# Two reorderings in a two-layer graph attention kernel: two reductions ahead of a waiting step on VectorE, and four coarse gathers ahead of two fine ones on GpSimd

## The chip, the cores and the metric

The kernel runs on one core of a Trainium2 chip. The metric is the device time of one execution in microseconds (us), as the median of several runs. A profiled execution gives, besides, the time of every instruction. Five engines work side by side, each through its own instructions in order: PE (matmul), DVE (vector), ACT (activation), POOL (GpSimd) and SP, which here only issues DMAs. They meet at semaphores. POOL issues the indirect DMAs.

## The reference, cut to what matters

There are 16 graphs ("batches") of 1024 nodes with 256 features, and one adjacency matrix for all. Layer 0 is a small network with two attentions, layer 1 one more attention, each with a layer norm in front and a residual:

```python
out = relu(h @ mlp1_w + mlp1_b)          # 1024 x 512
out = elu(gat(out, None, W_fc, a_fc)) + out       # dense: every node sees every node
out = relu(out @ mlp2_w + mlp2_b)        # 1024 x 256
x = x + relu(elu(gat(out, adj, W_hand, a_hand)) + out)
x = x + relu(gat1(relu(layernorm(x)), adj, W, a))
# gat: e = leaky_relu(f1[i] + f2[j]); softmax over j (of the neighbours); att @ h; elu
```

The change concerns how the dense attention gets its result, and when layer 1 computes two extremes.

## The kernel before, in words

**Dense attention without a 1024 x 1024 product.** The exponential of a leaky ReLU of f1[i] + f2[j] is one of two products of a function of i and a function of j, depending on whether f2[j] lies over -f1[i]. So the kernel sorts the nodes by f2 (it counts ranks and scatters the rows of `h_nat` to DRAM, `sorted`), makes running sums of the sorted rows from both ends, and reads for every node i the two sums at its place. The sums are held in two tables in DRAM: a fine one (`fine`, sums within groups of eight rows) and a coarse one (`coarse`, sums over whole groups, made by two triangular products `carry` on PE). A node's sum is its fine row plus its coarse row. `gather` (L627 on) fetches them: for a half h of the nodes (512, four tiles of 128) and a tile u, a fine gather writes 128 rows of 1026 floats into `got`, and a coarse gather adds 128 rows to the same place in flight:

```python
nc.gpsimd.indirect_dma_start(
    out=got[u // n][:, u % n, :], out_offset=None,
    in_=(coarse_d if coarse else fine_d)[self.b % 2][:, :],
    in_offset=bass.IndirectOffsetOnAxis(ap=self.k[:, coarse, t:t + 1], axis=0),
    **({"compute_op": OP.add} if coarse else {}))
```

So a batch has sixteen gathers, eight per half, and a coarse one waits until the fine one of its tile has landed. `share` (L649 to L652, DVE) turns the four sums of a half into weights `den`, and so waits for the last coarse gather of its half. `mean` makes per tile `part` on ACT (L659) and `hp` on DVE (L661). `merge` (L708 on) turns the four `hp` of a half by PE transposes `hpT`, four times (c = 0 to 3), applies the elu (L710 on DVE, L711 and L712 on ACT, L718 on DVE), and POOL adds the result to `resT` (L719). Then comes the second product, `m` at L726. `hp` has four buffers, so both halves share them.

**Layer 1 and its extremes.** For each batch, `second_norm` turns the normalised rows (`nt`, L282), `project` makes `hmb` (PE products `pb` at L322, ACT copies at L324, a POOL memset of a column of ones at L318), and `extremes` (L329, L330) takes the largest and smallest of a column of eight numbers on each partition. `vectors` begins with a PE transpose `extpsb` (L238) that spreads the largest over the partitions. In steady batches the weighted product `ob` of layer 1 follows in the next batch's time.

**What sets the order.** Every step is entered in a table with a planned time, by `at(lo, hi, steps)`. The steps are sorted by that time, and the instructions of PE, DVE, ACT and SP are issued in just this order. POOL keeps the order of the table too, but for the scatters. The planned times are only places in a list; nothing waits for a clock. Batches overlap: the sums, gathers and merges of batch b + 1 run while batch b is in its masked attention and layer 1. A batch's place in the table is `base`, 142 planned us from the next. For batches from the second to the last, the fine gathers stand at `base + 44.5` and `base + 48`, the coarse ones at `base + 55` and `base + 62`; the shares at `base + 78` and `base + 91.4`; the reductions at `lo + 7.5` with `lo = base + 71`. Between the gathers POOL has other work: the two adds `posa` (L408) and `ea` (L409) of each tile of the masked attention of layer 0, whose result DVE adds to x (L413), and the inverse root of the next norm (`rstd`, L267 and L268), on which the centring `hn` (L272) waits.

On SP, the store of a finished half of the output (L429) and the load of a later x (L86) are issued in the time of the coarse gathers. They go through another DMA queue to the same sixteen DMA engines.

## Time and profile before

| | us |
|---|---|
| three runs: median (lowest to highest) | 2363.75 (2357.47 to 2365.26) |
| the profiled execution, its own time | 2357.62 |
| its span, from the first to the last instruction | 2355.9 |
| PE busy | 2264.0 |
| DVE busy | 1610.9 |
| ACT busy | 1243.7 |
| POOL busy | 954.7 |
| a fine gather on POOL, a coarse one (median) | 0.96, 1.55 |
| from a gather's issue to its landing (median) | 8.1 |
| one extreme, L329 or L330 (DVE) | 0.16 |

A line of the timeline reads: start in us from the span's start, duration in us, engine, line of the code, operation, result <- operands, their shapes, how many were merged into the line, and in brackets how long the engine stood idle before it and what ended that. A line of waits reads: who waited, for whom, us in total, times, longest. Busy time on PE is partly modelled. What POOL shows of a gather is its issue; the transfer goes on afterwards in the DMA engines. The mean granted clock of PE was 0.990.

### The profile page before, as it was taken

To read this page: it belongs to the slowest core of one execution; us is meant where nothing else is said; L and a number is where in the kernel's file an instruction comes from. 1 tells how busy PE (TensorE), PEld (TensorE's weight loads), DVE (VectorE), ACT (ScalarE), POOL (GpSimd) and SP (SyncE) were. 2 spreads that over 40 slices of the span, in tenths; PEclk is the share of its full clock that TensorE was granted. 3 is DMA by queue.
4 is the path that set the end of the run, shared out by engine and by line. 5 is a ranking of instruction groups with operands and counts; after the bars stand their busy time and mean duration, and the time that the engine had idled before them with its cause. 6 is when DMAs were issued, how large, how long until landed. Compare 5 with 4: busy or idle time off the path is not lost. (4 is left out here: it accounts for less than half of the span.)

```text
span 2355.9 us, 30815 instructions
## 1 busy us (share of the span) xinstructions
PE 2264.0 (96%) x9955; PEld 1750.0 (74%) x9955; DVE 1610.9 (68%) x4499; ACT 1243.7 (53%) x2740; POOL 954.7 (41%) x1216
## 2 busy tenths in 40 slices
PE   8989999999999999999999999999999999999897
PEld 6666777777868778787877868777786877778676
DVE  6666685766858577685866767586685857668554
ACT  5355645647365564745546374554736556473442
POOL 1153435264433536434263533535344352634320
PEclk9999999999999999999999999999999999999898
DMA  4558356572655746366573645657264564636500
GB/s 175 166 161 206 74 167 172 168 189 96 191 127 175 184 149 183 96 193 151 170 188 128 178 112 173 163 170 201 96 196 118 171 179 152 184 95 193 122 1 29
DMA packets 150762, 355.81 MB, mean 151 GB/s; under 512 B 11112, under 2 KB 62648, under 8 KB 146496
## 3 DMA queue, kind: packets, MB, share of 16 engines
q1 hardware_dynamic: 103968, 189.58, 26.4%
q0 software_dynamic: 45952, 163.99, 26.3%
q8 instruction: 82, 1.34, 0.2%
q14 instruction: 88, 0.72, 0.1%
q10 hardware_dynamic: 672, 0.17, 0.0%
HBM read 227.40 MB, written 126.30 MB: 150 GB/s over the span
## 5 line engine op out<-in xcount | busy, mean ns | idle before, releaser
L384 PE MATMUL ob<-hmb,attb 128*128 128x257 f32 x2048 | 466.7, 386 | 13.6 <-DVE attb L373 13.5
L465 PE MATMUL h<-wfc_sb,resT 128*128 128x257 f32 x2048 | 465.5, 380 | 0.0
L384 PE MATMUL oa<-hma,atta 128*128 128x258 f32 x2048 | 454.4, 382 | 3.1 <-DVE atta L373 2.9
L384 PEld LDWEIGHTS ob<-hmb,attb 128*128 128x128 f32 x2048 | 388.3, 192 | 79.1 <-ACT rb L422 12.5
L384 PEld LDWEIGHTS oa<-hma,atta 128*128 128x128 f32 x2048 | 387.1, 190 | 65.1 <-DVE atta L373 9.6
L465 PEld LDWEIGHTS h<-wfc_sb,resT 128*128 128x128 f32 x2048 | 379.4, 190 | 53.5 <-issue 0.7
L719 POOL TENSOR_TENSOR resT<-resT,e 128x512 f32<-128x512 f32 x128 | 163.3, 1276 | 386.9 <-DVE e L718 343.4
L408 POOL TENSOR_TENSOR posa<-posa,onat 128x256 f32<-128x256 f32 x120 | 100.8, 840 | 468.2 <-ACT posa L400 467.6
L373 DVE SCALAR_TENSOR_TENSOR atta<-rowsa,qwda,edge 128x256 f32<-128x256 f32 x512 | 268.2, 554 | 24.0 <-PE oa L384 12.6
L373 DVE SCALAR_TENSOR_TENSOR attb<-rowsb,qwdb,edge 128x256 f32<-128x256 f32 x512 | 237.2, 505 | 9.9 <-PE ob L384 7.4
L451 PE MATMUL m<-hT,w_sb 128*128 128x512 f32 x512 | 236.2, 599 | 0.5 <-ACT posa L400 0.5
L726 PE MATMUL m<-resT,w_sb 128*128 128x512 f32 x512 | 231.5, 599 | 4.4 <-POOL resT L719 4.4
L422 ACT ACTIVATE rb<-ob,recb 128x256 f32<-128x256 f32 x128 | 59.1, 475 | 332.1 <-DVE recb L420 320.4
L637 POOL DMA_INDIRECT got<-coarse,k x124 | 198.1, 1598 | 39.0 <-issue 35.4
L399 ACT ACTIVATE ea<-oa,reca 128x256 f32<-128x256 f32 x128 | 60.8, 475 | 267.6 <-DVE reca L396 267.6
L710 DVE TENSOR_SCALAR e<-hpT 128x512 f32<-128x512 f32 x128 | 88.4, 690 | 141.3 <-PE hpT L708 108.8
L726 PEld LDWEIGHTS m<-resT,w_sb 128*128 128x128 f32 x512 | 94.1, 192 | 107.2 <-issue 91.3
L451 PEld LDWEIGHTS m<-hT,w_sb 128*128 128x128 f32 x512 | 93.0, 194 | 92.1 <-issue 89.7
L637 POOL DMA_INDIRECT got<-fine,k x124 | 128.9, 1040 | 55.4 <-DMA fine<-xs 23.9
L525 POOL DMA_INDIRECT sorted<-hnat,place x128 | 131.4, 1026 | 39.5 <-issue 20.3
L548 ACT ACTIVATE junk<-r,fs 128x1024 int8<-128x1024 f32 x124 | 142.4, 1149 | 5.7 <-POOL fs L469 4.7
L711 ACT ACTIVATE e<-e 128x512 f32<-128x512 f32 x128 | 80.7, 631 | 88.0 <-DVE e L710 87.9
(186 smaller groups left out, 3442.4 us busy)
## 6 DMA issues: line engine op xcount, KB each, us to landing
xs<-sorted SPq DMA_DIRECT2D x32, 1028.0 KB
fine<-tt SPq DMA_DIRECT2D x32, 1026.0 KB
fine<-xs SPq DMA_DIRECT2D x32, 1026.0 KB
x<-in_x_dram SPq DMA_DIRECT2D x16, 1024.0 KB
out_dram<-x SPq DMA_DIRECT2D x32, 512.0 KB
xn<-in_x_dram SPq DMA_DIRECT2D x15, 1024.0 KB
coarse<-carry SPq DMA_DIRECT2D x32, 256.5 KB
r<-row_r SPq DMA_DIRECT2D x14, 512.0 KB
```

What stands on the lines that cost most here:

```text
L373: nc.vector.scalar_tensor_tensor(a_t, self.rows[:, q * PAIR:(q + 1) * PAIR], self.qwd[:, 1, j:j + 1], edge[:, j, q * PAIR:(q + 1) * PAIR], ...
L384: nc.tensor.matmul(self.out[t][:, :F + self.ONES], lhsT=self.att[q, j][:, (t % 2) * P:(t % 2 + 1) * P], rhs=self.hm[:, j, 2:2 + F + self.O ...
L408: adder.tensor_add(pos, pos, o_nat[:, t, :])
L451: nc.tensor.matmul(ps, lhsT=w1_sb[:, kc, c * P:(c + 1) * P], rhs=hT[:, kc, h * HALF:(h + 1) * HALF], start=(kc == 0), stop=(kc == FC - 1))
L465: nc.tensor.matmul(ps[:, :F + 1], lhsT=self.resT[:, kc, t * P:(t + 1) * P], rhs=wfc_sb[:, kc, g, :], start=(kc == 0), stop=(kc == HC - 1))
L525: made = nc.gpsimd.indirect_dma_start(out=sorted_d[self.b % 2], out_offset=bass.IndirectOffsetOnAxis(ap=self.place[:, t:t + 1], axis=0), i ...
L548: nc.scalar.activation(junk, self.r2, AF.Sign, bias=self.fs[:, 0, t:t + 1], accum_out=self.signs[:, t:t + 1])
L637: nc.gpsimd.indirect_dma_start(out=got[u // n][:, u % n, :], out_offset=None, in_=(coarse_d if coarse else fine_d)[self.b % 2][:, :], in_o ...
L710: nc.vector.tensor_scalar_min(e, ps, 0.0)
L711: nc.scalar.activation(e, e, AF.Exp)
L719: nc.gpsimd.tensor_add(dst, dst, e)
L726: nc.tensor.matmul(ps, lhsT=w2_sb[:, kc, c * P:(c + 1) * P], rhs=self.resT[:, kc, h * HALF:(h + 1) * HALF], start=(kc == 0), stop=(kc == H ...
```

## The change

Two places of the table are moved. The reductions `extremes` go from `lo + 7.5` to `lo + 6.9`, which is just ahead of the first half's share instead of behind it and its first `hp`. The gathers of batches 2 to 15 (the first two batches keep theirs) are entered by a new function, `all_gathers`: first the four fine ones of the first half and two of the second, then the four coarse ones of the first half, the last two fine ones of the second half, and its four coarse ones.

```diff
+    def all_gathers(d, lo, hi):
+
+        at(lo, lo + 7, each(d.gather, [0], [0], range(TH)) + each(d.gather, [1], [0], range(2)))
+        at(hi, hi + 14, each(d.gather, [0], [1], range(TH))
+           + each(d.gather, [1], [0], range(2, TH)) + each(d.gather, [1], [1], range(TH)))
...
         at(lo, lo + 7, each(m.project, range(NT)))
-        at(lo + 7.5, lo + 7.5, [m.extremes])
+        at(lo + 6.9, lo + 6.9, [m.extremes])
...
-            for h in range(NH):
-                if b:
-                    gathers(dense[b + 1], h, base + 44.5 + 3.5 * h, base + 55 + 7 * h)
-                else:
+            if b:
+                all_gathers(dense[b + 1], base + 44.5, base + 55)
+            else:
+                for h in range(NH):
                     gathers(dense[1], h, base + 16 + 12 * h, base + 22 + 25 * h)
```

What this does to the order of the engines, in batches 2 to 15: on POOL the gathers stood, with f and c for fine and coarse and the half's number, as f0 f0 f0, adds of tile 6, f0, adds of tile 7, f1 f1 f1 f1, c0, root, c0 c0 c0, c1 c1 c1 c1; in batches 5 to 8 the first f1 stood ahead of the adds of tile 7. They now stand as f0 f0 f0, adds of tile 6, adds of tile 7, f0, f1 f1, c0 c0, root, c0 c0, f1 f1, c1 c1 c1 c1. On DVE the two reductions stand ahead of the first half's share in thirteen batches. The orders of PE, ACT and SP are the same as before.

## The prediction

> **What bounds the kernel now.** I read the page first, then the waits of the matmul engine, then the timeline of one steady batch on each engine, then the rate of the DMA engines in that batch.

> ```profile
> span 2355.9 us, 30815 instructions
> PE 2264.0 (96%) x9955; PEld 1750.0 (74%) x9955; DVE 1610.9 (68%) x4499; ACT 1243.7 (53%) x2740; POOL 954.7 (41%) x1216
> ```

> PE is busy 96% of the span: 92 us of idle time is all that a change of order can win. The waits of PE (us in total, times, longest) say where most of it is:

> ```profile
> PE extpsb L238 <- DVE extb L330: 22.0, 13, 2.7
> PE nt L282 <- DVE hn L272: 15.4, 8, 9.7
> PE ob L384 <- DVE attb L373: 13.5, 20, 2.1
> PE hpT L708 <- DVE hp L661: 6.4, 7, 1.7
> ```

> The first is what the change aims at: once a batch PE stops for two tiny reductions (`extb`). Batch 2 (I number by the batch whose gathers run) on DVE and PE shows why:

> ```profile
> 381.69 0.16 DVE L649 TENSOR_TENSOR den<-got,qd 128x4 f32<-128x4 f32 x1 [10.24 <-DMA got<-coarse,k]
> 383.25 0.75 DVE L661 SCALAR_TENSOR_TENSOR hp<-got,den,part 128x513 f32<-128x513 f32 x1 [0.79 <-ACT part L659]
> 383.92 0.16 DVE L329 TENSOR_REDUCE extb<-hmb 128x1 f32<-128x8 f32 x1
> 384.23 0.29 PE L238 MATMUL extpsb<-ident,extb 128*128 128x128 f32 x1 [2.48 <-DVE extb L330]
> ...
> 393.16 0.73 DVE L649 TENSOR_TENSOR den<-got,qd 128x4 f32<-128x4 f32 x1 [0.65 <-DMA got<-coarse,k]
> 397.17 2.97 DVE L661 SCALAR_TENSOR_TENSOR hp<-got,den,part 128x513 f32<-128x513 f32 x4 [1.47 <-ACT part L659]
> 400.25 0.60 PE L708 MATMUL hpT<-ident,hp 128*128 128x128 f32 x4
> ```

> DVE stands 10.24 us at the share of the first half until its last coarse gather lands; the reductions, whose input ACT finished copying at about 376, stand behind it. The last three lines matter as much: the second half's gathers land at 393.0, and the four `hp` that the second merge (`hpT`, h=1) needs end at 400.14, 0.1 us after PE arrives. PE comes without a wait **because** it was held 2.48 us before. The second half's data is as late as the first's.

> Batch 7 has no wait at `extpsb`, a sample of what happens then:

> ```profile
> 1081.60 0.29 PE L238 MATMUL extpsb<-ident,extb 128*128 128x128 f32 x1
> 1091.71 0.16 DVE L649 TENSOR_TENSOR den<-got,qd 128x4 f32<-128x4 f32 x1 [1.83 <-DMA got<-coarse,k]
> 1095.16 2.96 DVE L661 SCALAR_TENSOR_TENSOR hp<-got,den,part 128x513 f32<-128x513 f32 x4 [1.47 <-ACT part L659]
> 1097.62 0.89 PE L708 MATMUL hpT<-ident,hp 128*128 128x128 f32 x4
> ```

> PE came early, `hpT` took 0.89 instead of 0.60, and PE went on 0.22 us after the last `hp` (in the other batches 0.55).

> Last, batch 2 by stretches (busy us of PE, PEld, DVE, ACT, POOL; then PE's granted clock, the share of the 16 DMA engines' time, GB/s):

> ```profile
> 352.00:358.00 6.00, 6.00 (x29) 5.28 (x28) 1.95 (x6) 0.83 (x3) 5.25 (x7) 1.00 0.84 274
> 358.00:364.00 6.00, 5.65 (x30) 4.49 (x29) 5.93 (x20) 0.95 (x2) 4.74 (x5) 1.00 0.79 246
> 370.00:376.00 6.00, 6.00 (x30) 5.20 (x29) 0.49 (x2) 3.38 (x10) 5.02 (x4) 1.00 1.07 212
> 376.00:382.00 6.00, 5.75 (x15) 2.46 (x13) 0.28 (x2) 1.20 (x3) 3.21 (x3) 1.00 1.06 226
> ```

> During the fine gathers it has holes (0.79 to 0.84); from the coarse ones on it is full. By the landings, a coarse gather takes 2.5 us, 3.0 us once the next `xn` load and an output store share the engines; fine ones, when queued, follow each other by 1.3.

> [...]

> **The change, part by part.** PE, ACT and SP keep their orders; no work is added or removed.

> *Extremes.* Two reductions, 2 x 0.156 = 0.31 us, go from behind the first `hp` to ahead of the share, in batches 2 to 14 (13 times). Behind them on DVE stands the share, which waits for DMA anyway: cost nothing, 0.3 us if the data were already there. `extpsb` no longer waits on the gathers: 20.6 us over batches 2 to 14 leave this place. Behind it PE has 1.7 us of `mlp1` products, then the first merge, which needs four `hp`, done about 4.8 us after the landing. Alone this would hand the wait to the first merge.

> *Gathers, first half.* The four coarse ones are issued two fine slots earlier, 2 x 1.3 us. In DMA order two fines drop behind them: adding the transfer times above in the new order I get their end at f+27.9 instead of f+31.4 in batch 2 (f: the first fine gather, 349.86), 3.5 us earlier. The first merge then has its `hp` 4.8 later, at f+32.7; PE, no longer held at f+31.9 by `extpsb`, arrives at f+33.7. That wait is gone, with 1 us to spare.

> *Gathers, second half.* What counts is when the last coarse gather lands: f+43.1 before (42.4 to 43.8). The sixteen transfers are the same, so if DMA was full throughout it doesn't move. What can move it: the adds of tile 7 (1.5 us) now run right after those of tile 6, so fine 3 is issued 1.5 us later; the DMA hole there grows by as much as the hole after it shrinks. Against that, a coarse gather asks more of DMA (2.5 us) than its issue takes (1.95), so coarse ones put earlier fill the holes of 358 to 364. Between the landing of the fifth fine (f+13.4) and of the first coarse (f+22.5), 9.1 us, DMA had 3 x 1.3 + 2.5 + 1.6 (an output store) = 8.0 us to do; 1.1 us could be won. Bounds: 1.1 earlier to 0.6 later; I take 0.3 earlier, as latency rather than bandwidth may own part of the hole.

> *Added waits.* Coarse 2 and 3 of the second half now wait for fines issued just before: until about f+29.3 and f+30.8, where they were issued at f+26.4 and f+28.2. DMA still has two coarse gathers queued, so it doesn't run dry. Behind them on POOL stands the memset of `hmb`'s ones column, then `L719`, wanted at f+38: free, except in batch 15, where `L368` scales `hmb` at once (2193.07, memset ended 2192.29). There the memset ends near 2195.7: +2.6 us, some of it swallowed by PE's later waits: +2.3.

> *Tile 7's adds*, 1.3 to 2.7 us earlier, free DVE's update and so `attb` (13.5 us of waits); the normalisation's root stays at its time or 0.7 us earlier. This only lets PE reach the second merge sooner.

> **The sum.** From now on PE should wait at the second merge in every batch, as in batch 7: it goes on at landing + 6.54 + 0.22. Before it went on at landing + `hp` delay + about 0.55, where the delay was 6.69 to 7.86. The gains with an unmoved landing, batches 2 to 14: 0.89, 0.50, 0.49, 0.48, 0.50, 0, 0.52, 0.51, 0.50, 0.52, 0.50, 1.85, 0.64 = 8.4 us. Landing 0.3 earlier: 13 x 0.3 = 3.9. Batch 15: -2.3. In all 10.0 us. Against the profiled execution (2357.62 us, span 2355.9) this makes a span of 2345.9; that run is 6 us under the median, so the same gain from the median 2363.75 gives 2353.75, say 2353.5. So half of the 20.6 us is won; the rest moves to the second merge.

> **The rivals.** *All of it is won.* If DMA had been held by latency and late issue, the last landing comes 1.1 us earlier or more: 8.4 + 14.3 - 2.3 = 20, the size of the wait: 2343. For it: the 0.79. Against: 1.06 from 376 on, with a fixed list of transfers. *It only changes its place.* The landing comes 0.2 later, or the gain of the hand-over is smaller than batch 7 suggests: 8.4 - 2.6 - 2.3 = 3.5 us or less: 2360. For it: the balance of both halves in every batch. *The DMA hole decides, slower.* Fine 3's 1.5 us delay isn't filled; the landing comes 1.5 later: 8.4 - 19.5 - 2.3 = -13: 2377. It turns slower beyond 0.5 us (8.4 - 2.3 = 6.1 over 13). For it: nothing is queued at DMA then. Against: batches 5 to 8 issue fine 4 1.4 us sooner and land just the same (43.0 against 43.1).

> **How the numbers follow.** About 0.3% (7.1 us) is what a measurement can tell. My sum 0.45, all 0.16, change of place 0.25, hole 0.14. Of my sum's cases (landing 0 to 0.8 earlier, 6 to 16 us) nine in ten pass 7.1: faster 0.45 x 0.9 + 0.16 + a little of the third = 0.59; slower: most of the hole's, 0.13; same 0.28. My sum's own range is 2347 to 2358; for 8 in 10 I add all of the first rival and the third, and leave out most of the hole: 2341 to 2367.

> **What would show it.** Right: `extpsb` gone from the waits; `hpT <- hp` up from 6.4 to about 20 us (28 us of PE's idle time lies between carry and second merge in batches 2 to 14; 12 of it are won, most of the rest goes there); the first share about 3.5 us earlier against f, the second 0 to 1; `L649` at 0.16; `ob <- attb` down; PE idle near 82. Wrong: a last landing more than 0.5 us later, a first merge that waits, or a second merge that doesn't, and then the gain is 20.

## The result: 0.46% slower, not 0.4% faster

| | before | changed |
|---|---|---|
| median of 11 runs each on one chip, us | 2363.75 (2357.47 to 2366.12) | 2373.3 (2366.97 to 2382.73) |
| ratio to before | | 1.0046, 95% interval 1.0033 to 1.0059 |
| the profiled execution, its span, us | 2357.62, 2355.9 | 2379.36, 2377.5 |
| its mean granted PE clock | 0.990 | 0.985 |

Predicted were 2353.5 us and a range of 2341 to 2367; the median lies 20 us above the one and 6 us beyond the other. The profiled execution of the changed kernel is one of its longer ones, so I take sizes from the medians and means of runs, and places from the trace. The description of the change holds for batches 2 to 4 and 9 to 15 only: in batches 5 to 8 of the changed kernel the last `f0` still stands ahead of the adds of tile 7, as the first `f1` had before.

The page of the changed kernel, the same two lines:

```profile
span 2377.5 us, 30843 instructions
PE 2280.7 (96%) x9955; PEld 1760.7 (74%) x9955; DVE 1617.7 (68%) x4499; ACT 1242.8 (52%) x2740; POOL 966.3 (41%) x1216
```

PE's idle time is 96.8 us (2377.5 - 2280.7) where it was 91.9: 5 us more. But its *busy* time, for the same 9955 matmuls, rose by 16.7 us. So most of this execution's loss stands as busy time and not as idle time. Two things are in it, and both show below: a halved clock (0.50 for 3.41 us at a time), and transposes that run one at a time and count as busier than the same ones in a row (1.29 us for 0.60 in batch 2).

The waits of PE (us in total, times, longest):

```profile
PE hpT L708 <- DVE hp L661: 33.6, 59, 1.7
PE nt L282 <- DVE hn L272: 15.4, 8, 9.7
PE ob L384 <- DVE attb L373: 5.4, 6, 2.1
PE ob L384 <- ACT hmb L368: 4.9, 1, 4.9
...
PE extpsb L238 <- DVE extb L330: 1.5, 2, 0.8
```

`extpsb` has gone from 22.0 to 1.5 and `ob <- attb` from 13.5 to 5.4, as foreseen. `hpT <- hp` has gone from 6.4 to 33.6, not to about 20: 26.5 of it stand at the second merge of batches 2 to 14, where there was 0.1. `ob <- hmb` is new; it is batch 15.

Batch 2 of the changed kernel (f, its first fine gather, is at 352.90), first DVE:

```profile
380.80 0.16 DVE L649 TENSOR_TENSOR den<-got,qd 128x4 f32<-128x4 f32 x1 [1.23 <-DMA got<-coarse,k]
...
396.37 0.17 DVE L649 TENSOR_TENSOR den<-got,qd 128x4 f32<-128x4 f32 x1 [4.39 <-DMA got<-coarse,k]
...
399.82 2.96 DVE L661 SCALAR_TENSOR_TENSOR hp<-got,den,part 128x513 f32<-128x513 f32 x4 [1.47 <-ACT part L659]
```

then PE:

```profile
383.87 0.27 PE L238 MATMUL extpsb<-ident,extb 128*128 128x128 f32 x1
...
400.72 0.30 PE L708 MATMUL hpT<-ident,hp 128*128 128x128 f32 x1 [0.84 <-DVE hp L661]
401.29 0.33 PE L708 MATMUL hpT<-ident,hp 128*128 128x128 f32 x1 [0.27 <-DVE hp L661]
402.17 0.33 PE L708 MATMUL hpT<-ident,hp 128*128 128x128 f32 x1 [0.55 <-DVE hp L661]
402.84 0.33 PE L708 MATMUL hpT<-ident,hp 128*128 128x128 f32 x1 [0.34 <-DVE hp L661]
403.00 1.31 PE L465 MATMUL h<-wfc_sb,resT 128*128 128x257 f32 x3
```

The first half's share starts at f+27.90 instead of f+31.83, `extpsb` doesn't wait, and the second half's share starts at f+43.46 instead of f+43.30. PE reaches the second merge at 399.88 and then takes the four `hp` one at a time as DVE makes them: four gaps, 2.0 us in sum, around four short transposes. One by one these count as 1.29 us busy (0.30 and three times 0.33), where four in a row take 0.60.

What comes next is the part that the prediction had no step for. The changed kernel by stretches (busy us of PE, PEld, DVE, ACT, POOL; PE's granted clock; DMA share; GB/s), around that merge:

```profile
399.75:403.15 3.40, 1.40 (x6) 0.73 (x6) 3.20 (x5) 3.06 (x9) 0.00 (x0) 1.00 0.00 0
403.16:406.57 3.41, 3.41 (x11) 2.60 (x10) 0.82 (x2) 1.66 (x4) 1.27 (x1) 0.50 0.01 1
406.57:410.00 3.43, 3.43 (x12) 1.76 (x11) 1.29 (x2) 1.65 (x3) 1.27 (x1) 1.00 0.00 0
```

and the kernel before around the same merge (PE at 400.25, no wait):

```profile
396.79:400.20 3.41, 3.41 (x18) 2.97 (x17) 2.90 (x5) 3.07 (x8) 0.27 (x1) 1.00 0.00 0
400.20:403.60 3.40, 3.40 (x19) 2.72 (x18) 1.70 (x3) 2.24 (x5) 1.27 (x1) 1.00 0.01 1
```

In the stretch with the gaps PE is busy 1.40 of 3.40 us. The next 3.41 us are granted at 0.50: PE is fully busy and gets less done. Eight `h` (L465) take 3.30 us in it, 0.41 each, where one takes 0.23 in the whole trace (474.1 us for 2048). By the granted clock that costs 1.7 us, half of 3.41, on top of the 2.0 us of gaps. Then the clock is back. In batches 2 to 14 the trace of before has one such stretch of 3.41 us, that of the changed kernel seven (at 403.2, 546.5, 1109.7, 1393.0, two in a row at 1672.9, and 1816.3), each beginning inside a second merge or less than 1 us behind it, the second of the two in a row apart.

The mean granted clock is recorded for every run, so this can be priced without relying on one execution. I take a run's time, times one minus its clock, as what it lost to the clock, and the remainder as what it would take at full clock. (That is the most it can have lost: a halved clock counts here even where PE had nothing to do.) Over all its runs the changed kernel loses 34.1 us to the clock and the kernel before 26.4 and 27.2 us (27 and 32 runs beside the experiments below). So of the 11 us between the means (2374.1 and 2362.9) about 7 are clock and about 4 are other time. Where the clock is lost, only the traces tell: in the profiled executions before and changed lose 5.1 and 5.1 us ahead of batch 2's first share, 1.7 and 11.9 us in batches 2 to 14, and 17.7 and 20.6 us behind them. So in this pair some 10 of 13 us of the difference belong to batches 2 to 14. Most of what either kernel loses lies at the two ends.

Last, the DMA side of batch 2, at the same distances from f as in the prediction's fence (f+2.1, f+8.1, f+20.1, f+26.1):

```profile
355.04:361.04 6.00, 6.00 (x29) 5.27 (x28) 3.97 (x10) 1.02 (x4) 5.08 (x7) 1.00 0.69 252
361.04:367.04 6.00, 6.00 (x34) 5.31 (x33) 5.93 (x21) 0.76 (x2) 5.07 (x4) 1.00 0.81 228
...
373.04:379.04 6.00, 6.00 (x28) 5.11 (x27) 0.42 (x1) 2.87 (x9) 4.78 (x5) 1.00 1.06 213
379.04:385.04 6.00, 6.00 (x16) 2.72 (x15) 3.46 (x10) 4.17 (x8) 2.70 (x3) 1.00 1.02 309
```

The holes are no smaller: 0.69 and 0.81 against 0.84 and 0.79. And where DMA was full with coarse gathers (1.06 at 226 GB/s) it now moves 309 GB/s at 1.02: the fine gathers that were moved behind run beside the `xn` load, which SP issues at about f+22. Over batches 2 to 14 the last landing (the start of the second share less the 0.12 us between the two) is at f+43.84, against f+43.11.

### The profile page after: what moved, and what is told of

Same layout as the page of the kernel before. It is cut to its first block, busy times and chain, and to the rows that moved or that the text cites. A ratio compares the mean times of both kernels' runs of the same rounds, so it can differ in the third digit from the quotient of the medians.

```text
span 2377.5 us, 30843 instructions
## 1 busy us (share of the span) xinstructions
PE 2280.7 (96%) x9955; PEld 1760.7 (74%) x9955; DVE 1617.7 (68%) x4499; ACT 1242.8 (52%) x2740; POOL 966.3 (41%) x1216
## 3 DMA queue, kind: packets, MB, share of 16 engines
q1 hardware_dynamic: 103968, 189.58, 27.2%
q0 software_dynamic: 45952, 163.99, 26.1%
## 5 line engine op out<-in xcount | busy, mean ns | idle before, releaser
L465 PE MATMUL h<-wfc_sb,resT 128*128 128x257 f32 x2048 | 474.1, 385 | 0.0
L384 PE MATMUL ob<-hmb,attb 128*128 128x257 f32 x2048 | 461.7, 384 | 10.3 <-DVE attb L373 5.4
L384 PE MATMUL oa<-hma,atta 128*128 128x258 f32 x2048 | 457.4, 383 | 4.6 <-DVE atta L373 4.4
L384 PEld LDWEIGHTS ob<-hmb,attb 128*128 128x128 f32 x2048 | 390.1, 192 | 69.1 <-ACT hmb L368 6.9
L384 PEld LDWEIGHTS oa<-hma,atta 128*128 128x128 f32 x2048 | 387.9, 190 | 69.2 <-DVE atta L373 11.4
L465 PEld LDWEIGHTS h<-wfc_sb,resT 128*128 128x128 f32 x2048 | 384.7, 193 | 55.3 <-issue 0.7
L719 POOL TENSOR_TENSOR resT<-resT,e 128x512 f32<-128x512 f32 x128 | 163.1, 1274 | 333.8 <-DVE e L718 290.3
L373 DVE SCALAR_TENSOR_TENSOR atta<-rowsa,qwda,edge 128x256 f32<-128x256 f32 x512 | 268.1, 553 | 29.5 <-PE oa L384 14.3
L373 DVE SCALAR_TENSOR_TENSOR attb<-rowsb,qwdb,edge 128x256 f32<-128x256 f32 x512 | 241.7, 514 | 11.0 <-PE ob L384 8.4
L637 POOL DMA_INDIRECT got<-coarse,k x124 | 209.2, 1687 | 91.8 <-DMA got<-fine,k 58.0
L525 POOL DMA_INDIRECT sorted<-hnat,place x128 | 131.3, 1026 | 39.4 <-issue 19.8
```

Source lines behind the costliest of these rows:

```text
L373: nc.vector.scalar_tensor_tensor(a_t, self.rows[:, q * PAIR:(q + 1) * PAIR], self.qwd[:, 1, j:j + 1], edge[:, j, q * PAIR:(q + 1) * PAIR], ...
L384: nc.tensor.matmul(self.out[t][:, :F + self.ONES], lhsT=self.att[q, j][:, (t % 2) * P:(t % 2 + 1) * P], rhs=self.hm[:, j, 2:2 + F + self.O ...
L465: nc.tensor.matmul(ps[:, :F + 1], lhsT=self.resT[:, kc, t * P:(t + 1) * P], rhs=wfc_sb[:, kc, g, :], start=(kc == 0), stop=(kc == HC - 1))
L525: made = nc.gpsimd.indirect_dma_start(out=sorted_d[self.b % 2], out_offset=bass.IndirectOffsetOnAxis(ap=self.place[:, t:t + 1], axis=0), i ...
L637: nc.gpsimd.indirect_dma_start(out=got[u // n][:, u % n, :], out_offset=None, in_=(coarse_d if coarse else fine_d)[self.b % 2][:, :], in_o ...
L719: nc.gpsimd.tensor_add(dst, dst, e)
```

## The experiments

Two theories to be told apart, each with a rival. **Clock**: gaps at the second merge cost more than their length, because PE's clock is halved after them; rival: the busy time rose for other reasons, and only the wait counts. **Landing**: the last landing sets the end, and it comes later because SP's transfers (the `xn` load, 1 MB) share the DMA engines with the gathers that were moved behind; rival, the prediction's third: the fine gather delayed behind the adds of tile 7 leaves a hole.

All ten results in one table. Landings are means over batches 2 to 14 of the profiled execution, in us from f. The two waits are sums over the same batches: `extpsb` with the first merge, and the second merge. Clock and rest are means over all runs of the kernel. In the three groups of runs the kernel before had medians of 2361.7 (e1 to e4), 2362.1 (e5 to e8) and 2359.2 (e9, e10).

| kernel | median | ratio to before | first, last landing | waits | lost to clock | rest |
|---|---|---|---|---|---|---|
| before | | | 31.2, 43.1 | 20.6, 0.1 | 26.4; 27.2; 23.4 | 2335.6; 2334.8; 2335.7 |
| changed | 2373.30 | 1.0046 (1.0033 to 1.0059) | 28.7, 43.8 | 0.9, 26.5 | 34.1 | 2340.0 |
| e1 extremes only | 2359.32 | 0.9988 (0.9977 to 0.9999) | 31.3, 43.2 | 15.2, 0.0 | 25.1 | 2334.0 |
| e2 gathers only | 2373.46 | 1.0052 (1.0032 to 1.0073) | 28.3, 43.6 | 1.1, 23.6 | 32.8 | 2339.7 |
| e3 changed, merge filled | 2361.34 | 0.9999 (0.9984 to 1.0013) | 28.5, 43.6 | 0.9, 3.9 | 21.1 | 2340.5 |
| e4 changed, late `xn` | 2345.82 | 0.9931 (0.9915 to 0.9948) | 28.5, 42.2 | 0.3, 11.1 | 25.0 | 2320.4 |
| e5 before, late `xn` | 2360.97 | 0.9999 (0.9986 to 1.0011) | 31.1, 42.2 | 19.8, 0.0 | 26.1 | 2335.0 |
| e6 late `xn`, filled | 2343.74 | 0.9922 (0.9907 to 0.9936) | 28.7, 42.5 | 1.2, 0.0 | 19.2 | 2324.6 |
| e7 changed, fine 3 early | 2371.73 | 1.0037 (1.0027 to 1.0048) | 28.9, 44.0 | 0.3, 19.4 | 30.7 | 2340.6 |
| e8 late `xn` and store, filled | 2340.12 | 0.9910 (0.9895 to 0.9925) | 28.1, 41.0 | 0.0, 0.0 | 17.3 | 2323.3 |
| e9 late `xn` and store | 2326.87 | 0.9853 (0.9829 to 0.9878) | 28.0, 40.9 | 0.3, 1.2 | 23.7 | 2301.9 |
| e10 old order, late `xn` and store | 2344.66 | 0.9936 (0.9914 to 0.9959) | 30.6, 41.3 | 8.7, 0.0 | 18.8 | 2325.5 |

### e1 and e2: each half of the change alone

e1 is the kernel before with

```diff
-        at(lo + 7.5, lo + 7.5, [m.extremes])
+        at(lo + 6.9, lo + 6.9, [m.extremes])
```

> The reductions moved, the gathers in the order of before. Theory A (the change loses through the PE clock: its wait at a merge, broken up by single transposes, lets the clock drop to half for 3.4 us): the landings are those of before (last one at f+43.1), the 20 us of waiting go from the transpose of the extremes to the first merge, where they are broken up too, so 3 to 7 half-clock windows between batches 2 and 14 instead of 1 and 0 to 0.4% over before. Theory B (the change loses only because the second half's gathers land 0.7 us later): within 0.2% of before, or 4 us faster, with no more half-clock windows than before.

e2 is the changed kernel with the extremes put back to `lo + 7.5`.

> The gathers moved, the reductions where they were before. Both theories: the first half lands about 3 us earlier, so the reductions are done before PE wants them even behind the share, and the last landing is at f+43.8. Then the wait sits at the second merge as with both parts, and the time is that of the change within 0.2% (2368 to 2378). If instead the reductions are what costs, the time is that of before (2360 to 2366).

Their waits of PE, first e1:

```profile
PE hpT L708 <- DVE hp L661: 21.6, 42, 1.7
```

then e2:

```profile
PE hpT L708 <- DVE hp L661: 30.2, 56, 1.7
```

The extremes alone do what the prediction said they would alone: `extpsb` stops waiting and the first merge waits instead, 15.2 us of the 20.6. That is worth 0.12%, with an interval that nearly touches 1. In fact the whole wait has moved: the list counts the gaps alone, but with the lone transposes between them the first merge holds PE for 2.17 us a batch instead of 0.51, which makes 21.6 us. At 1.2 us of gaps a batch no price of the clock shows: over its runs e1 loses 25.1 us to it, no more than the kernel before, although its profiled execution, one of its longest, has three half-clock stretches in batches 2 to 14.

The gathers alone are the whole loss. With them `extpsb` hardly waits even where the extremes stand in the old place (1.1 us), since the first half lands 2.9 us earlier. In the new order of the gathers the extremes have nothing left to win.

### e3: fill the gaps of the second merge

The changed kernel, with products that nobody reads put among the four transposes of the second merge in batches 2 to 15 (the transposes then write over their place in `hpT`):

```diff
             for u in range(TH):
+                if self.b >= 2 and h == 1 and c == 0:
+                    for n in ((HALF,), (P,), (P, P), (P,))[u]:
+                        at_u = ps[:, :HALF] if n == HALF else ps[:, u * P:(u + 1) * P]
+                        nc.tensor.matmul(at_u, lhsT=w1_sb[:, 0, :P], rhs=w1_sb[:, 0, :n],
+                                         start=True, stop=True)
                 nc.tensor.transpose(ps[:, u * P:(u + 1) * P], self.hps[h, u][:, lo:lo + P], ident)
```

> The changed kernel with five products of constants, 1.7 us of PE work whose result is overwritten, put among the four transposes that wait at the second merge (batches 2 to 15). Nothing waits less. Theory A: PE counts as busy, the 7 half-clock windows between batches 2 and 14 fall to 2 or fewer, and 8 to 12 us come back: 2361 to 2366. Theory B: the landings are as late as before, so 2371 to 2376, or some us more for the added work.

PE in batch 2 of e3 (f is at 350.47):

```profile
397.82 1.02 PE L711 MATMUL hpT<-w_sb 128*128 128x512 f32 x2
398.68 0.28 PE L713 MATMUL hpT<-ident,hp 128*128 128x128 f32 x1
398.80 0.39 PE L711 MATMUL hpT<-w_sb 128*128 128x128 f32 x2
399.30 0.33 PE L713 MATMUL hpT<-ident,hp 128*128 128x128 f32 x1
399.46 0.61 PE L711 MATMUL hpT<-w_sb 128*128 128x128 f32 x4
```

PE does strictly more work than in the changed kernel, its last landing comes only 0.2 us earlier, and the time falls by 12 us, back to that of before. The table says where: 13.0 us less lost to the clock (34.1 to 21.1), and a rest that is the same within 0.5 us (2340.0 and 2340.5). No half-clock stretch is left in batches 2 to 14 of its trace. This shows that the gaps of the second merge cost clock. But the products stand in batch 15 too, and of the 18 us less that its trace loses to the clock, 12 lie in batches 2 to 14 and 6 behind them. So it is luck that the time comes out just as before: what remains of the loss, about 5 us of later landing and batch 15, is covered by clock that the kernel before loses too (by the traces 1.7 us in batches 2 to 14 and 3.3 behind them).

### e4: keep the next load out of the gathers' way

The changed kernel, with the `xn` load of batches 4 and up issued only when the last gather has landed:

```diff
         xn[b] = load_x(b, "xn")
+        if b >= 4:
+            wait_for(load_x.made, dense[b - 2].gathered, "behind the gathers")
```

> The changed kernel with the load of a later x (1 MB, batches 4 to 15) held until the last gather of its time has landed, instead of running beside the coarse gathers. Both theories say that the landing is what PE waits for at the second merge. [...] the last landing comes 1.4 to 2.5 us earlier (f+41.3 to 42.4, as in batch 14 of the change, which has no such load), the second merge waits 0.5 to 1 us instead of 2, half-clock windows fall to 2 or fewer, and the time is 2340 to 2352. If issue on GpSimd or latency sets the landing, it stays at f+43.8 and the time at 2370 or over.

PE in batch 2 of e4 (f is at 349.52):

```profile
396.49 0.50 PE L708 MATMUL hpT<-ident,hp 128*128 128x128 f32 x2
397.55 0.33 PE L708 MATMUL hpT<-ident,hp 128*128 128x128 f32 x1 [0.55 <-DVE hp L661]
398.21 0.33 PE L708 MATMUL hpT<-ident,hp 128*128 128x128 f32 x1 [0.34 <-DVE hp L661]
```

The last landing comes 1.6 us earlier than in the changed kernel, within the 1.4 to 2.5 of the theory **Landing**; 13 x 1.6 = 21 us, and the rest falls by 19.6. Two of the four gaps are gone, the wait is 0.9 us a batch, and the loss to the clock falls by 9.1 us as well. So the last landing sets the time of the changed kernel, and a microsecond of it is worth more than a microsecond.

### e5: the same late load in the kernel before

The same edit on the kernel before.

> The kernel before, with one edit: the xn load of the batch behind (1 MB, batches 4 and up) is issued only when the last gather has landed. Theory 'the loads share the engines with the gathers, whatever the order of the gathers': the last landing comes 0.7 to 1.3 us earlier than f+43.1, the first half's landing too (f+30.5 or so instead of 31.2), extpsb waits about 10 us instead of 20.6, and the time is 8 to 13 us below the kernel before, about 2350. Rival 'the load only gets in the way because the changed order runs the fine gathers beside it': landings as before (31.2 and 43.1), time within 3 us of the kernel before, about 2361. The old order with the late load should in any case stay behind the new order with the late load (2345.8), as here the first half's landing still stops PE at extpsb.

Its wait at `extpsb`:

```profile
PE extpsb L238 <- DVE extb L330: 21.3, 13, 2.6
```

The last landing comes 0.9 us earlier, as expected, and the time does not move: I had expected 8 to 13 us, and that was wrong. The first half's landing hardly moved (31.2 to 31.1), so PE is held at `extpsb` as before (22.0, 21.3) and reaches the second merge as late as before. In the old order, with the extremes in their old place, the *first* half's landing is the bound, and the 0.9 us by which the second half comes earlier turn into slack.

With e4 it makes a square. With the load out of the way the last landing is at f+42.2 in either order. With the load among the gathers it is f+43.1 in the old order and f+43.8 in the new. So, with the load out of the way, the order of the gathers moves the last landing by nothing; it makes the load cost 1.6 us instead of 0.9.

### e7: the fourth fine gather back in its place

```diff
-        at(lo, lo + 7, each(d.gather, [0], [0], range(TH)) + each(d.gather, [1], [0], range(2)))
+        at(lo, lo + 4, each(d.gather, [0], [0], range(TH)))
+        at(lo + 3.5, lo + 5.5, each(d.gather, [1], [0], range(2)))
```

In every batch the fourth fine gather now stands ahead of the adds of tile 7 (in batches 5 to 8 the fifth as well); the rest is the changed kernel.

> The changed kernel, but the fourth fine gather stands ahead of the adds of tile 7 again in every batch, as before the change (the rest of the new order stays). Theory 'the xn load beside the fine gathers makes the last landing later, not the gap in the issues': last landing still f+43.6 to 44.3, time as the changed kernel, 2368 to 2375. Rival 'the hole of the delayed fourth fine gather makes it later' (the prediction's third rival): landing back at f+43.1 or less, second merge's wait 9 us shorter in sum, time about 2360.

Its wait at `ob`:

```profile
PE ob L384 <- DVE attb L373: 12.5, 19, 2.1
```

The last landing is at f+44.0, no earlier than 43.8, and the time is that of the changed kernel. The second merge does wait 7 us less (19.4 for 26.5), but not because its data come sooner: `ob <- attb`, which had fallen from 13.5 to 5.4 with the early adds of tile 7, is back at 12.5, and PE comes to the merge later. The hole behind the adds, the prediction's third rival, is not the cause. Batches 5 to 8 of the changed kernel had said so already: there the gather was never delayed, and they land at f+43.9 to f+44.8.

### e6 and e8: all of it together, and the store as well

e6 is e4 with the filling of e3 in it, and with batch 15's gathers in the order of before:

```diff
-            if b:
+            if b and b + 2 < NB:
                 all_gathers(dense[b + 1], base + 44.5, base + 55)
+            elif b:
+                for h in range(NH):
+                    gathers(dense[b + 1], h, base + 44.5 + 3.5 * h, base + 55 + 7 * h)
```

> The change with the late xn load (2345.8 alone), the dummy products in the second merge of batches 2 to 14, and batch 15's gathers in the order of before. Theory 'the memset behind the late gathers costs batch 15 1.3 to 2.6 us, and a wait at the merge costs clock only where it is long': the wait of ob for hmb's scaling is gone (4.9 us in the changed kernel), the second merge's wait in the trace falls from 11 us to about 3, and the time is 1 to 4 us below 2345.8, about 2343. Rival 'the half-clock stretches come with any wait': some 2338, as no stretch is left. Rival 'the products cost as much as they save': 2346 or more.

The wait of `ob` for `hmb` is gone from e6's list, and its time is 2343.74, where 2343 was expected. But the composition is not what was expected: against e4 it loses 5.8 us less to the clock, and the rest is 4.2 us *more*. The products last longer than the wait that is left for them (11.1 us in e4), so they now hold PE up: it goes on 7.06 us behind the last landing in the mean, where it was 6.76 in e4. That is 4 us over 13 batches; a landing 0.2 us later makes some 3 more.

e8 is e6 with the output store of a batch's second half also held until the last gather has landed:

```diff
+            if h and b + 2 < NB:
+                wait_for(made, dense[b + 2].gathered, "behind the gathers")
```

> As the kernel with the late xn load, the products and batch 15 in the old order, and in addition the output store of a batch's second half (1 MB) is held until the last gather has landed (batches with gathers behind them). Theory 'what the SP queue moves before the last landing sets that landing': it comes a further 0.5 to 1.5 us earlier (f+41 to 41.7 instead of 42.24), the second merge waits for next to nothing, and the time is 5 to 12 us below that kernel, about 2335. Rival 'without the load the gathers are bound by GpSimd's issue and the transfers' latency': landing stays at f+42.0 to 42.3, time the same within 2 us.

(The store is of 0.5 MB, not of 1 MB as I wrote there.) The last landing moved by a further 1.5 us, to f+41.0, so it is SP's traffic and not GpSimd's issue that sets it. Only 3.6 us of that came through, less than the 5 to 12 expected: with no wait left at the second merge, PE is bound by its own work, the products among it.

### e9 and e10: without the products, and in the old order

e9 is e8 without the products.

> The kernel with late xn load, late store and batch 15's gathers in the old order, without the dummy products. Theory 'with the last landing at f+41 the second merge hardly waits, so there is nothing left to fill and the dummy products only cost PE's time': the second merge's wait stays under 0.4 us a batch, PE's mean clock over the runs stays at 0.990 or above, and the time is 4 to 10 us below the kernel with the products (2340.1), about 2334. Rival 'the products keep the clock up whatever waits there are': the clock falls to 0.988 or less and the time is 2340 or more.

PE in batch 2 of e9 (f is at 354.20), around the first merge, and its longest waits:

```profile
385.16 0.27 PE L238 MATMUL extpsb<-ident,extb 128*128 128x128 f32 x1
385.27 1.88 PE L454 MATMUL m<-hT,w_sb 128*128 128x512 f32 x4
386.99 0.60 PE L711 MATMUL hpT<-ident,hp 128*128 128x128 f32 x4
```

```profile
PE nt L282 <- DVE hn L272: 15.5, 8, 9.8
PE hpT L711 <- DVE hp L664: 7.6, 11, 1.7
PE ob L384 <- DVE attb L373: 7.4, 8, 2.1
```

2326.87 us: 1.47% below the kernel before, the best of all. Neither the extremes nor the merges hold PE any more. The gain over e8 is 13.3 us where 4 to 10 were expected. The rest falls by 21.4 us, which fits the 1.47 us a batch by which PE's way from `carry` past the second merge is shorter than in e8; and 6.4 us of it go back to the clock (17.3 to 23.7). The rival said that the products keep the clock up whatever waits there are. It asked for a clock of 0.988 or less and a time of 2340 or more; the mean clock was 0.990. For the merges of batches 2 to 14 it is not borne out either: neither e8 nor e9 has a half-clock stretch there in its trace. The difference of the two traces lies behind batch 14 (13.3 us lost in e8, 20.6 in e9). Whether the products of batch 15 make it is not shown; e10, which has none, loses 12.6 us there.

e10 is the kernel before with the extremes moved and both transfers late: the same as e9 but for the order of the gathers.

> The order of the gathers of before, the extremes ahead of the share, and both the xn load and the output store held until the last gather has landed. Theory 'in the old order the first half's landing binds PE at the first merge, so an earlier last landing is worth little there': the first merge waits 0.7 to 1.2 us a batch, the last landing comes at f+41 to 41.5, and the time is 2350 to 2357. Rival 'the gathers' order does not matter once the SP queue stays out of the way': first merge without a wait, about 2336, as the kernel in the new order.

Its waits of PE:

```profile
PE nt L282 <- DVE hn L272: 15.5, 8, 9.8
PE hpT L711 <- DVE hp L664: 15.3, 29, 1.7
PE ob L384 <- DVE attb L373: 13.2, 19, 2.1
```

2344.66 us, between the two expectations. The first merge waits 0.67 us a batch, as the first half lands at f+30.6 and not at f+28.0. With its lone transposes it holds PE for 1.49 instead of 0.49 us, 13 us over the batches. Another 5.8 us are `ob <- attb` (13.2 for 7.4), since the new order also runs the adds of tile 7 earlier. These two make 19 of the 23.6 us between the rests (2325.5 and 2301.9); e10 gets 5 back from the clock. So the reordering on POOL, which costs about 14 us where SP's transfers run among the gathers (e1 against the changed kernel, 1.0046 - 0.9988), is worth 17.8 us (2344.66 - 2326.87) where they do not. The last landing itself is then 0.35 us earlier in the new order (40.93 for 41.28).

## Why the prediction was wrong, point by point

- **The extremes**: right. `extpsb`'s 20.6 us left that place, at no visible cost; alone the wait goes to the first merge (e1).
- **The first half's landing** and a first merge without a wait: right. f+27.8 in batch 2 (27.9 predicted), f+28.7 on average; the first merge waits 0.9 us in sum.
- **Two readings of the lines.** The fourth `hp` of batch 2 ends at 400.14 and PE begins the second merge at 400.25: the data were ready 0.1 us before PE came and not 0.1 after. That they were nearly late together stays true, and the argument rests on that. The last copy that the reductions wait for ends at 377.0 and not at about 376.
- **The hand-over** at the second merge, "landing + 6.54 + 0.22": right to the hundredth in 11 of 13 batches. The list of its thirteen gains adds up to 7.9, not to 8.4; 7.1 us came of it.
- **The second half's landing: this step failed.** It was bounded from 1.1 earlier to 0.6 later, taken as 0.3 earlier; it came 0.7 later. Instead of -3.9 us this is +9.4 over the 13 batches. The step reasoned with a fixed list of transfers and a full DMA, and it gave the hardware queue's transfers the same place in either order. But by moving two fine gathers behind the first coarse ones it put them beside the `xn` load. By e4 and e5 the load then costs 1.6 us of the last landing instead of 0.9. That the delay of fine 3 does it, as the third rival had it, is refuted by e7; that rival had the sign and nearly the time (2377), but by luck, for a wrong reason.
- **Batch 15**: the mechanism is right, the size roughly. POOL, ACT and PE of the changed kernel:

```profile
2214.22 0.71 POOL L318 MEMSET hmb<- 128x8 f32 x1
```

```profile
2214.96 3.31 ACT L368 ACTIVATE hmb<-hmb,qwdb 128x257 f32<-128x257 f32 x8 [3.27 <-POOL hmb L318]
```

```profile
2215.52 2.94 PE L384 MATMUL ob<-hmb,attb 128*128 128x257 f32 x6 [4.88 <-ACT hmb L368]
```

  PE's 4.88 us stand where before 1.71 us were waited for `attb`. From `carry` past the second merge the batch took 64.36 instead of 63.07 us: +1.3, where +2.3 was charged.
- **The step that was missing** is the clock. The sum took a wait at the second merge at its length. There PE waits in four gaps around four transposes, and a halved clock for 3.41 us follows often enough (behind six of the thirteen second merges of the profiled execution) to lose about 7 us more over the whole. The traces of before and changed have 10 and 16 halved stretches. Each is at 0.50, and lasts 3.413 us or two or three times that (the one cut by the span's end apart); within a trace their starts lie whole multiples of 3.413 us apart. Batch 7, the one sample of the new state, could not have warned of it: there PE's four transposes took only 0.29 us longer than in a row (0.89 for 0.60), and no half clock followed.
- **`L649`**, for which 0.16 us was given as a sign: right. Of the 32 in the trace of before, the 11 that ran while POOL had `L719` took 0.31 to 0.74 us, the other 21 took 0.14 to 0.17. In the changed kernel only one ran beside it (0.75), and the other 31 took 0.14 to 0.17. Why they take longer then, no run here tells.

The sum, with what the two profiled executions show: hand-over -7.1, landing +9.4, and a first gather that is issued 0.09 us later behind `carry`, +1.2, make +3.4 us in batches 2 to 14 (PE's way from `carry` past the second merge is 54.19 instead of 53.93 us). With batch 15 it is +4.7, against the 4.4 to 5.2 us that the runs show besides the clock. With some 7 us of clock it is about +12 instead of -10; the means lie 11 apart. The signs to look for were met in `extpsb`, in the first share, in L649 (0.17 us) and in `ob <- attb`; PE's idle time was 96.8 and not 82, and the last landing was in the region that the prediction had named as its refutation ("more than 0.5 us later").

**Open**: how the load comes to cost 0.7 us more in the new order. Adding up the DMA records, SP's queue moves 1879 KB before the last landing instead of 1777 (5.95 us of all engines' time instead of 5.73), while the gathers' own 34.2 us stay. That is 0.2 of the 0.7; the other 0.5 is time in which the engines are not full, and no run here tells why. SP also issues the load earlier, at f+21.3 instead of f+22.1 in most batches. This alone is not the cause: in e7 it is issued at f+22.1, as before, and the last landing is still at f+44.0.

## What to carry to other kernels

A wait that is moved to a place where PE is stopped several times in short succession costs its length and perhaps a halved clock behind it (here 1.8 to 2.4 us of gaps in batches 2 to 13, and behind six of these twelve merges 3.41 us or twice that at 0.50): look at the granted clock beside each wait, and compare PE's busy time for the same instructions. A list of waits counts only the gaps: short instructions between them stretch the same stop further (in e1 1.2 us of gaps a batch, and PE held for 2.17). When transfers are reordered, ask what else runs on the same DMA engines at the new time. Here holding back a load and a store that nobody was waiting for turned a loss of 0.46% into a gain of 1.47% (with batch 15's gathers back in the old order). Neither part does it alone: in the old order holding them back is worth 0.5% (e1 to e10), and the new order alone loses.

## What the runs showed of the hardware

**The price rises with the wait.** Ordered by the second merge's wait (11.1, 19.4, 23.6, 26.5 us in e4, e7, e2 and the changed kernel), the loss to the clock is 25.0, 30.7, 32.8 and 34.1 us. At 0.9 us a batch nothing is lost beyond what the kernel before loses, at 1.5 us some 4 us, at 2.0 us some 7. These are losses of whole runs; by the traces 26 to 29 us of each lie outside batches 2 to 14 and vary too, so the order is firmer than the steps.

**What an SP transfer costs the gathers.** Without the `xn` load the last gather lands 0.9 to 1.6 us earlier (e5, e4), without the store of the second half another 0.9 to 1.5 (e5 to e10, e6 to e8). The load moves 1 MB, 0.75 to 0.85 MB of it before the last landing, the store 0.5 MB. By the DMA records of SP's queue before the last landing, the load takes 2.4 us (before, 5.73 less 3.37 in e5) to 2.8 us (changed, 5.95 less 3.18 in e4) of all sixteen engines' time, and the store 1.7 to 1.8 us (3.18 less 1.51 in e9, 3.37 less 1.58 in e10).
